# x loaded in two pieces by blocks, its first statistics taken piece by piece, the count of small norms placed behind the narrow products, and one scaling of rows on GpSimd

## The chip, the cores and the metric

The kernel runs on one core of one Trainium2 chip. Its metric is the time of an execution on the device in microseconds (us). TensorE, VectorE, ScalarE and GpSimd are called PE, DVE, ACT and POOL in the profile; SP is the sync engine, which here only issues DMAs. PEld is the loading of weights on PE.

## What is computed

Four graph layers on x (3327 nodes, 64 features) and a sparse adjacency matrix, each followed by x = layernorm(x + layer(x)). Only the start and layer 1 bear on this change. Cut to that:

```
def _L0_gnn_ref(t, x, A):
    outer = R_CONST * jnp.sum(x * (A @ x), axis=1, keepdims=True)
    return F_CONST - B_CONST * x - outer          # + x, then a layernorm
def _L1_gnn_ref(x, adj, att_W, att_b):
    x_tan = _logmap0(x, C)
    left  = x_tan @ att_W[:D] + att_b
    right = x_tan @ att_W[D:]
    adj_att = jax.nn.sigmoid(left + right.T) * adj
    x_local = _logmap(x[:, None, :], x[None, :, :], C)
    support_t = jnp.einsum('ij,ijd->id', adj_att, x_local)
    return _proj(_expmap(x, support_t, C), C)
```

The terms of layer 0 that are the same for all features of a node vanish in its layernorm, so layer 0 costs only the centring and the variance of x, and no pass over the adjacency matrix. Layer 1 needs a logarithm and a sigmoid for every pair of nodes.

## The kernel before, in words

**Tiles.** The nodes are padded to 3328 = 26 blocks of 128. A block lies on the 128 partitions; `x0`, `xc` (x less its mean) and `lj` hold 26 slots of 64 features each, 1664 numbers per partition. Slot 2c holds block c and slot 2c+1 block c+13, so that a pair of slots can be transposed as one 128x128 square. So "the even slots" are the first 13 blocks and "the odd slots" the last 13.

**The start (L105 to L214, and L1202 to L1287).** Two DMAs bring x, the first 13 blocks on SP's queue and the last 13 on ACT's (L106). SP then issues short columns (`attw_dg`, `attb_sb`), two rows of blocks of the adjacency matrix (`keep`, L144) and weights. POOL and DVE build constants. PE fills the time with matmuls into `idle` whose result nobody reads (L1206, three of them, two instructions each since the type is float32). When x is there, each engine follows the order in which the code is written (`manual_schedule`):

- DVE: row sums of the even slots and of the odd (L1212), then `xc` of the even and of the odd (L1214), later the row sums of the squares (L1243), then the small statistics `vq`, `low`, `lows`, `root`, `t`, `r2`, `lf`, `rb`, `gas` on 128x26 numbers (L1244 to L1286).
- POOL: `lj`, each feature less the last one, from `x0` for the even slots and from `xc` for the odd ones (L1220).
- PE: 13 transposes of x in four groups of 4, 4, 4 and 1 (L1231); in the second group also `pw` (L1236), the centred attention weights. Then 13 products `pr` of a transposed block with the 4 columns of weights (L1258, two instructions each), with a matmul into `idle` after the first and the last group (L1264).
- ACT: copies of the transposes out of PSUM to `xT` (L1240); in the second group first a copy of `pw` and the two squares of `xc` (L1239).

**The count.** `lows` counts, per partition, the nodes whose variance is under a bound; a matmul with ones (L1256, `n_low`) adds them over partitions, DVE turns the sum into an integer `flag` (L1272), and every engine reads that into a register and branches on it (L2097, L2098): layer 1 is `near_sphere` where no node is below, and a general path otherwise. `n_low` stands in PE's order before the last group of `pr`, and `flag` in DVE's before `t`, `r2`, `lf`, `rb` and `gas`.

**Layer 1's start (L1520 to L1600).** On DVE `scaled` (L1540) multiplies `lj` by `gas`, slots 18 to 25, then 10 to 17, then 0 to 9, with `rows_of_i` (L1513) between. A copy of one number, `after` (L1554), makes POOL wait for the last of them. PE transposes `lf`, `lj` and `ri` (`left`, `right`, `turn`, `wrong`), and ACT and DVE copy these out (L1502) to `lb`, `ljT`, `riT`. Then a loop over 104 tiles (52 pairs): ACT takes a sigmoid of `lb` (L1360) and an arctangent of the products (L1396), POOL multiplies the sigmoid by the adjacency (L1365), DVE makes the weights `v` (L1407 to L1411), PE makes the products `pq` (L1387) and the sums `acc` (L1431). The first four pairs use adjacency blocks that are already in SBUF, the others are loaded by SP (`at`, L1334). The first pair's sigmoid and its multiplication are cut in two.

After the loop come the end of layer 1, and layers 2 and 3 (`layers`), bound by PE and by loads of the adjacency. The diff doesn't touch these.

Of the kernel before, what the change touches and what calls it, by code (L numbers as in the profile page):

```python
# [10 lines left out]
F32 = mybir.dt.float32  # L11
# [3 lines left out]
AF = mybir.ActivationFunctionType  # L15
ALU = mybir.AluOpType
AX = mybir.AxisListType
PSUM = bass.MemoryType.PSUM

P = 128  # L20
# [3 lines left out]
D = 64  # L24
CW = 416
HALF = NP // 2
NBH = NB // 2
# [55 lines left out]
def kernel(  # L83
# [11 lines left out]
    nc = tc.nc  # L95
# [6 lines left out]


    x0 = xpool.tile([P, NB, D], F32, tag="x", name="x0")
    for h, queue in enumerate((nc.sync, nc.scalar)):  # L105
        queue.dma_start(  # L106
            x0[:, h::2, :], x_in[h * HALF : (h + 1) * HALF].rearrange("(c p) d -> p c d", p=P)
        )

    ident = const.tile([P, P], F32, name="ident")  # L110
    make_identity(nc, ident)
    lj = const.tile([P, NB, D], F32, name="lj")
# [9 lines left out]
    ones = const.tile([P, 1], F32, name="ones")  # L122
# [19 lines left out]
    def keep(blocks):  # L142
        for jb in blocks:
            nc.sync.dma_start(kept[jb], adjT[jb * P : (jb + 1) * P, :])  # L144
# [53 lines left out]
    center_4 = center.unsqueeze(1).to_broadcast([P, 4, P])  # L198
# [30 lines left out]
    def stat(tag):  # L229
        return small.tile([P, NB], F32, tag=tag, name=tag)  # L230
# [43 lines left out]
    def by_half(v):  # L274

        return v.rearrange("p (n h) d -> p n h d", h=2)
# [900 lines left out]
    with tc.tile_pool(name="l1", bufs=1) as l1:  # L1177

        def l1_stat(name):
            return l1.tile([P, NB], F32, name=name)  # L1180
# [5 lines left out]
        s, inv_s, gas, lf, rb = (l1_stat(name) for name in ("s", "inv_s", "gas", "lf", "rb"))  # L1186
# [6 lines left out]
        xc = xpool.tile([P, NB, D], F32, tag="x", name="xc")  # L1193
        vec, sca = nc.vector.tensor_tensor, nc.vector.tensor_scalar
        stt = nc.vector.scalar_tensor_tensor
        with tc.tile_pool(name="l1a", bufs=1) as l1a, tc.tile_pool(
            name="l1ap", bufs=1, space=PSUM
        ) as l1ap:
            v = l1a.tile([P, NB], F32, name="v")
            sums = l1a.tile([P, NB], F32, name="sums")  # L1200
            sq = l1a.tile([P, NB, D], F32, name="sq_c")
            xT = l1a.tile([P, HALF], F32, name="xT_0")  # L1202

            idle = l1ap.tile([P, 4 * P], F32, name="idle")
            for _ in range(3):
                nc.tensor.matmul(idle, ident, center_4, start=True, stop=True)  # L1206

            pw = l1ap.tile([P, 4], F32, name="pw")
            attw_c = l1a.tile([P, 4], F32, name="attw_c")
            halves = (slice(0, None, 2), slice(1, None, 2))  # L1210
            for h in halves:
                nc.vector.tensor_reduce(sums[:, h], x0[:, h, :], axis=AX.X, op=ALU.add)  # L1212
            for h in halves:
                stt(  # L1214
                    xc[:, h, :], sums[:, h].unsqueeze(2).to_broadcast([P, NBH, D]), -1.0 / D,
                    x0[:, h, :], op0=ALU.mult, op1=ALU.add,
                )
            for h, c in zip(halves, (x0, xc)):

                nc.gpsimd.tensor_tensor(  # L1220
                    lj[:, h, : D - 1], c[:, h, : D - 1],
                    c[:, h, D - 1 : D].to_broadcast([P, NBH, D - 1]), ALU.subtract,
                )

            pr = l1ap.tile([P, NBH, 2, 2], F32, name="pr")
            turned = []
            for i, g in enumerate(range(0, NBH, 4)):
                n = min(4, NBH - g)
                pt = l1ap.tile([P, 4 * P], F32, tag="pt", bufs=4, name=f"pt_x_{g}")
                for k in range(n):  # L1230
                    nc.tensor.transpose(  # L1231
                        pt[:, k * P : (k + 1) * P],
                        by_half(x0)[:, g + k].rearrange("p h d -> p (h d)"), ident,
                    )
                if i == 1:
                    nc.tensor.matmul(pw, center, attw_dg, start=True, stop=True)  # L1236
                    nc.scalar.copy(attw_c, pw)
                    for h in halves:
                        nc.scalar.activation(sq[:, h, :], xc[:, h, :], AF.Square)  # L1239
                nc.scalar.copy(xT[:, g * P : (g + n) * P], pt[:, : n * P])  # L1240
                turned.append((g, n))
            for h in halves:
                nc.vector.tensor_reduce(v[:, h], sq[:, h, :], axis=AX.X, op=ALU.add)  # L1243
            sca(vq[:, 1], v, 0.81 / D, LN_EPS, ALU.mult, ALU.add)  # L1244
            sca(vq[:, 0], v, MIN_VAR, None, ALU.max)
            sca(vq[:, 2], v, 0.81 / D - 0.81, LN_EPS, ALU.mult, ALU.add)

            low = stat("low")
            stt(low, v, NEAR_VAR, real, op0=ALU.is_lt, op1=ALU.mult)
            lows = small.tile([P, 1], F32, tag="lows", name="lows")  # L1250
            nc.vector.tensor_reduce(lows, low, axis=AX.X, op=ALU.add)
            root = l1a.tile([P, 2, NB], F32, name="root")
            n_low = l1ap.tile([1, 1], F32, name="n_low")
            for i, (g, n) in enumerate(turned):
                if i == 3:
                    nc.tensor.matmul(n_low, lows, ones, start=True, stop=True)  # L1256
                for k in range(g, g + n):
                    nc.tensor.matmul(  # L1258
                        pr[:, k].rearrange("p h t -> p (h t)"), xT[:, k * P : (k + 1) * P],
                        attw_c, start=True, stop=True,  # L1260
                    )
                if i in (0, 3):
                    w = 2 if i else 4
                    nc.tensor.matmul(  # L1264
                        idle[:, : w * P], ident, center_4[:, :w], start=True, stop=True
                    )
            nc.scalar.activation(root, vq[:, :2], AF.Sqrt)
            nc.scalar.activation(warm, ones, AF.Sigmoid)
            nc.vector.reciprocal(root, root)
            t = l1a.tile([P, 2, NB], F32, name="t")  # L1270
            vec(t, vq[:, :2], root, ALU.mult)
            nc.vector.tensor_copy(flag, n_low)  # L1272
            vec(t, t, root, ALU.mult)
            stt(r2, t, -3.0, root, op0=ALU.add, op1=ALU.mult)
            prs = pr.rearrange("p n h t -> p (n h) t")
            stt(lf, prs[:, :, 0], -0.5 * LOG_NORM, r2[:, 0], op0=ALU.mult, op1=ALU.mult)
            stt(rb, prs[:, :, 1], -0.5 * LOG_NORM, r2[:, 0], op0=ALU.mult, op1=ALU.mult)

            nc.vector.reciprocal(rq, vq[:, 1:])
            sca(rb, rb, attb_sb, None, ALU.add)  # L1280
            sca(s, r2[:, 1], -0.45, None, ALU.mult)
            vec(g1, vq[:, 2], rq[:, 0], ALU.mult)
            vec(ga, vq[:, 1], rq[:, 1], ALU.mult)
            vec(gas, ga, s, ALU.mult)
            sca(lj[:, :, D - 1], ga, 2.0, -1.0, ALU.mult, ALU.add)
            sca(aa, g1, -1.0, 1.0, ALU.mult, ALU.add)  # L1286
        in_order.close()  # L1287

        def near_sphere(mT, ljT_0, xm, sq_e, t_e):
# [3 lines left out]
            with tc.tile_pool(name="n1", bufs=1, reuse_waits="tile") as n1, tc.tile_pool(  # L1293
                name="n1w", bufs=2, reuse_waits="tile"
            ) as n1w, tc.tile_pool(
                name="n1c", bufs=1, space=PSUM, reuse_waits="tile"
# [43 lines left out]
                pqs, accs, changes, sums = {}, {}, [], []  # L1340
# [170 lines left out]
                def rows_of_i(first, last):  # L1511
                    sl = slice(2 * first, 2 * last)
                    stt(  # L1513
                        ri[:, sl, : D - 1], xc[:, sl, : D - 1], -2.0,
                        gas[:, sl].unsqueeze(2).to_broadcast([P, sl.stop - sl.start, D - 1]),
                        op0=ALU.mult, op1=ALU.mult,
                    )
# [11 lines left out]
                with tc.manual_schedule(  # L1529
# [4 lines left out]
                ):  # L1534
                    copy = nc.vector.tensor_copy
                    keep((NB - 3, NB - 4))
                    def scaled(b, n):

                        sl = slice(2 * b, 2 * (b + n))
                        vec(  # L1540
                            lj[:, sl, : D - 1], lj[:, sl, : D - 1],
                            gas[:, sl].unsqueeze(2).to_broadcast([P, 2 * n, D - 1]), ALU.mult,
                        )
# [4 lines left out]
                    rows_of_i(4, 8)  # L1548
                    scaled(5, 4)
                    rows_of_i(8, NBH)  # L1550
                    scaled(0, 5)

                    after = n1.tile([P, 1], F32, name="after")
                    nc.gpsimd.tensor_copy(after, lj[:, 0, :1])  # L1554
                    spread_a, spread_b = bank(0, left, 0, 4), bank(1, left, 13, 4)
                    spread_a()
                    spread_b()
# [2 lines left out]
                    start = attention(0)  # L1560
# [38 lines left out]
                    for t in range(len(tiles)):  # L1599
# [23 lines left out]
                        if t == len(tiles) - 3:  # L1623
                            pq = n1q.tile([P, 2, 512], F32, tag="pq", name="pq_early")
                            pm = pq[:, :, : 3 * (P + 2)].rearrange("p a (k w) -> p a k w", k=3)
                            for b in range(6):
                                nc.tensor.matmul(
                                    pm[:, b // 3, b % 3], mT[:, b * P : (b + 1) * P], all_m,
                                    start=True, stop=True,
# [524 lines left out]
```

## Time and profile before

| | us |
|---|---|
| three runs: median (lowest to highest) | 500.58 (498.72 to 500.65) |
| the profiled execution | 499.99 |
| its span | 498.2 |
| x asked for, first used by DVE, both halves used by PE | 0.81, 6.25, 7.14 |
| `n_low` on PE, `flag` on DVE | 14.53, 14.76 |
| PE's first instruction of layer 1, ACT's first, first arctangent | 16.37, 17.59, 24.52 |
| first loads of layer 2's stream, after the pair loop | 192.13 |

Times within an execution count from the span's start. A busy share of a stage says little by itself: what is read is which wait ended last ahead of an instruction. In a row of the timeline the columns are the start, the time to the end of the last of the instructions that are merged in the row, the engine, the line, what it writes and reads, and in brackets how long the engine had been idle and what ended that. Matmuls overlap, so the distance of two starts, not a duration, tells their pace.

### The profile page before, as it was taken

The numbers are of one execution on the slowest core, as the hardware profiler recorded it, in microseconds if no ns is written. First come the engines' busy times: TensorE is split into PE (matmuls) and PEld (weight loads), VectorE is DVE, ScalarE is ACT, GpSimd is POOL, SyncE is SP. The second block draws the span as 40 slices with busy tenths as digits, with TensorE's granted clock in tenths as the row PEclk, the third lists the DMA queues.
The fourth block names the chain that finished last, engine by engine and source line by source line (L and its number), as shares of the span: only waits on it lengthen the run. The fifth ranks groups of instructions, "written<-read, shape, count | busy, mean of one in ns | idle before, by whom it ended". The sixth has DMA issues, their size and how long they took to land. (4 is left out here: it accounts for less than half of the span.)

```text
span 498.2 us, 7727 instructions
## 1 busy us (share of the span) xinstructions
PE 480.3 (96%) x2865; PEld 220.4 (44%) x2865; DVE 349.5 (70%) x602; ACT 266.1 (53%) x377; POOL 192.1 (39%) x171
## 2 busy tenths in 40 slices
PE   7999999999999999999999999999999999999992
PEld 4733333333333338643333353333345554455551
DVE  6788888878888887995363322656239998788744
ACT  4799999999999985300000000000016885657541
POOL 4299999989999991000000000000242154000000
PEclk9799999999999998999999999999999999999996
DMA  9888988887888278899999019998987699949001
GB/s 278 340 284 285 328 265 274 273 272 259 283 274 277 72 285 312 365 402 428 424 425 379 0 22 393 430 362 325 414 337 236 224 331 364 392 162 357 3 1 43
DMA packets 34202, 139.20 MB, mean 279 GB/s; under 512 B 11263, under 2 KB 13041, under 8 KB 29035
## 3 DMA queue, kind: packets, MB, share of 16 engines
q1 hardware_dynamic: 30603, 137.41, 73.8%
q0 software_dynamic: 1216, 0.63, 0.6%
q10 hardware_dynamic: 2336, 0.58, 0.6%
q8 instruction: 24, 0.39, 0.3%
q14 instruction: 23, 0.19, 0.1%
HBM read 136.93 MB, written 1.04 MB: 277 GB/s over the span
## 5 line engine op out<-in xcount | busy, mean ns | idle before, releaser
L1365 POOL TENSOR_TENSOR sg<-sg,at 128x832 f32<-128x832 f32 x88 | 131.4, 1517 | 7.7 <-ACT sg L1360 3.7
L517 PE MATMUL cnt<-at_l,lj 128*64 128x416 f32 x496 | 90.8, 515 | 0.8 <-DMA at_l<-in_adjT 0.8
L1360 ACT ACTIVATE sg<-lb,rb 128x1664 f32<-128x1664 f32 (+1 forms) x53 | 88.1, 1664 | 0.0
L1387 PE MATMUL pq<-riT,ljT 64*128 64x416 f32 x416 | 87.4, 536 | 0.2
L1431 PE MATMUL acc<-v,lj 128*64 128x416 f32 x416 | 85.2, 525 | 0.0
L1396 ACT ACTIVATE pq<-pq 128x832 f32<-128x832 f32 x104 | 83.8, 851 | 1.8 <-issue 1.6
L630 ACT ACTIVATE x<-cnt 128x416 f32<-128x416 f32 x8 | 4.1, 517 | 144.7 <-PE cnt L517 144.7
L669 ACT ACTIVATE w<-cnt 128x416 int16<-128x416 f32 x136 | 63.9, 522 | 25.3 <-PE cnt L651 23.8
L1411 DVE SCALAR_TENSOR_TENSOR v<-pq,sg 128x832 f32<-128x832 f32 x52 | 53.3, 1025 | 19.0 <-ACT pq L1396 18.6
L464 POOL DMA_DIRECT2D t_rows<-tb x4 | 2.7, 720 | 151.0 <-DVE tb L462 151.0
L1387 PEld LDWEIGHTS pq<-riT,ljT 64*128 64x128 f32 x416 | 35.5, 186 | 49.8 <-ACT pq L1396 30.6
L517 PEld LDWEIGHTS cnt<-at_l,lj 128*64 128x64 f32 x496 | 34.3, 137 | 51.0 <-issue 48.4
L882 PE MATMUL acc<-w,s 128*128 128x416 bf16 x208 | 53.1, 339 | 0.0
L1431 PEld LDWEIGHTS acc<-v,lj 128*64 128x64 f32 x416 | 26.1, 136 | 52.3 <-issue 48.2
L667 DVE TENSOR_SCALAR w<-cnt 128x416 int16<-128x416 f32 x72 | 41.6, 587 | 10.0 <-PE cnt L651 7.8
L517 PE MATMUL cnt<-kept,lj 128*64 128x416 f32 x224 | 41.6, 514 | 0.0
L651 PE MATMUL cnt<-mask,tri 128*128 128x416 bf16 x136 | 35.5, 339 | 1.8 <-ACT w L669 0.9
L368 DVE TENSOR_SCALAR mask<-ah 128x1664 bf16<-128x1664 f32 x34 | 35.5, 1060 | 2.3 <-DMA ah<-in_adjT 2.3
L1408 DVE SCALAR_TENSOR_TENSOR pq<-pq,sg 128x416 f32<-128x416 f32 x52 | 31.2, 600 | 1.8
L445 DVE TENSOR_SCALAR tm<-at_l 128x1664 bf16<-128x1664 f32 x16 | 15.7, 1023 | 22.9 <-PE t L452 20.9
L1407 DVE SCALAR_TENSOR_TENSOR v<-pq,sg 128x416 f32<-128x416 f32 x52 | 30.2, 581 | 0.0
L1035 POOL DMA_DIRECT2D out<-hid x1 | 0.5, 502 | 74.5 <-DVE hid L1040 74.5
(320 smaller groups left out, 523.5 us busy)
## 6 DMA issues: line engine op xcount, KB each, us to landing
at_l<-in_adjT SPq DMA_DIRECT2D x27, 1664.0 KB
at<-in_adjT SPq DMA_DIRECT2D x44, 832.0 KB
ah<-in_adjT SPq DMA_DIRECT2D x34, 832.0 KB
kept<-in_adjT SPq DMA_DIRECT2D x7, 1664.0 KB
bt_l<-in_adjT SPq DMA_DIRECT2D x6, 1664.0 KB
lb<-lf_rows SPq DMA_DIRECT2D x2, 384.0 KB
mask<-t_rows SPq DMA_DIRECT2D x34, 3.2 KB
ljT<-ljT SPq DMA_DIRECT2D x4, 128.0 KB
```

Of the source, the lines that this page charges most:

```text
L368: nc.vector.tensor_scalar(mask[q], ahead.pop(q), 0.0, None, ALU.not_equal)
L517: nc.tensor.matmul(acc[c][h * D : (h + 1) * D, :], hw[:, slot(jb), :], blocks[jb][:, o : o + CW], start=c not in begun, stop=last, skip_gr ...
L651: nc.tensor.matmul(cnt[c][e], tri, mask[q][:, of], start=True, stop=True, skip_group_check=True,)
L667: nc.vector.tensor_scalar(to, of, 0.0, None, ALU.max)
L669: nc.scalar.activation(to, of, AF.Relu)
L882: nc.tensor.matmul(acc[h, c][:, e, :], s12[:, slot(jb)].rearrange("p t d -> p (t d)"), ws[q, c, e], start=first, stop=last,)
L1360: nc.scalar.activation(sg[:, :, of], lbs[:, :, of], AF.Sigmoid, bias=rb[:, sl : sl + 1])
L1365: nc.gpsimd.tensor_tensor(sg[:, h, of], sg[:, h, of], at[:, h, of], ALU.mult)
L1387: nc.tensor.matmul(pq[:, h, :], ljT[h != jb // NBH][rows, of], riT[rows, ch * CW : (ch + 1) * CW], start=True, stop=True,)
L1396: nc.scalar.activation(pqs[t], pqs[t], AF.Arctan, bias=ANGLE_FIRST, scale=ANGLE_STEP)
L1411: stt(w, pq, ANGLE_REST, sg, op0=ALU.add, op1=ALU.mult)
L1431: nc.tensor.matmul(accs[cp, ci][h * D : (h + 1) * D, :], lj[:, slot(jb), :], w[:, h, :], start=(jb == orders[cp][0]), stop=(jb == orders[c ...
```

## The change

x comes in two pieces by blocks: blocks 0 to 6 and 13 to 19 (slots 0 to 13), then blocks 7 to 12 and 20 to 25 (slots 14 to 25), each piece as one DMA on SP and one on ACT. Sums, `xc`, `lj`, the squares and their sums go by these pieces instead of by even and odd slots, with the sum and `xc` of the first piece ahead of the second's, and the second square behind the second copy to `xT`. Two of three `idle` matmuls ahead of x are dropped. `n_low` stands behind the last group of `pr`. `scaled(0, 5)` goes to POOL, and `after` is dropped.

```diff
-    for h, queue in enumerate((nc.sync, nc.scalar)):
-        queue.dma_start(
-            x0[:, h::2, :], x_in[h * HALF : (h + 1) * HALF].rearrange("(c p) d -> p c d", p=P)
-        )
+    x_parts = (slice(0, 7), slice(7, NBH))
+    for s in x_parts:
+        for h, queue in enumerate((nc.sync, nc.scalar)):
+            o = h * HALF
+            queue.dma_start(
+                x0[:, 2 * s.start + h : 2 * s.stop : 2, :],
+                x_in[o + s.start * P : o + s.stop * P].rearrange("(c p) d -> p c d", p=P),
+            )
...
-            for _ in range(3):
-                nc.tensor.matmul(idle, ident, center_4, start=True, stop=True)
+            nc.tensor.matmul(idle, ident, center_4, start=True, stop=True)
...
-            halves = (slice(0, None, 2), slice(1, None, 2))
-            for h in halves:
-                nc.vector.tensor_reduce(sums[:, h], x0[:, h, :], axis=AX.X, op=ALU.add)
-            for h in halves:
+            pieces = [slice(2 * p.start, 2 * p.stop) for p in x_parts]
+            for sl in pieces:
+                nc.vector.tensor_reduce(sums[:, sl], x0[:, sl, :], axis=AX.X, op=ALU.add)
                 stt(
-                    xc[:, h, :], sums[:, h].unsqueeze(2).to_broadcast([P, NBH, D]), -1.0 / D,
-                    x0[:, h, :], op0=ALU.mult, op1=ALU.add,
+                    xc[:, sl, :],
+                    sums[:, sl].unsqueeze(2).to_broadcast([P, sl.stop - sl.start, D]), -1.0 / D,
+                    x0[:, sl, :], op0=ALU.mult, op1=ALU.add,
                 )
-            for h, c in zip(halves, (x0, xc)):
+            for sl, c in zip(pieces, (x0, xc)):
...
-                    for h in halves:
-                        nc.scalar.activation(sq[:, h, :], xc[:, h, :], AF.Square)
+                if i in (1, 2):
+                    sl = pieces[i - 1]
+                    nc.scalar.activation(sq[:, sl, :], xc[:, sl, :], AF.Square)
                 nc.scalar.copy(xT[:, g * P : (g + n) * P], pt[:, : n * P])
...
-            for h in halves:
-                nc.vector.tensor_reduce(v[:, h], sq[:, h, :], axis=AX.X, op=ALU.add)
+            for sl in pieces:
+                nc.vector.tensor_reduce(v[:, sl], sq[:, sl, :], axis=AX.X, op=ALU.add)
...
-                if i == 3:
-                    nc.tensor.matmul(n_low, lows, ones, start=True, stop=True)
                 for k in range(g, g + n):
                     nc.tensor.matmul(
                         pr[:, k].rearrange("p h t -> p (h t)"), xT[:, k * P : (k + 1) * P],
                         attw_c, start=True, stop=True,
                     )
+                if i == 3:
+                    nc.tensor.matmul(n_low, lows, ones, start=True, stop=True)
...
-                    def scaled(b, n):
+                    def scaled(b, n, engine=nc.vector):
...
-                        vec(
+                        engine.tensor_tensor(
...
-                    scaled(0, 5)
-
-                    after = n1.tile([P, 1], F32, name="after")
-                    nc.gpsimd.tensor_copy(after, lj[:, 0, :1])
+                    scaled(0, 5, nc.gpsimd)
```

More of the change, by code (lines that the diff above doesn't have):

```diff
@@ L1204 @@
             idle = l1ap.tile([P, 4 * P], F32, name="idle")
-            for _ in range(3):
-                nc.tensor.matmul(idle, ident, center_4, start=True, stop=True)
+            nc.tensor.matmul(idle, ident, center_4, start=True, stop=True)
             pw = l1ap.tile([P, 4], F32, name="pw")
             attw_c = l1a.tile([P, 4], F32, name="attw_c")
-            halves = (slice(0, None, 2), slice(1, None, 2))
-            for h in halves:
-                nc.vector.tensor_reduce(sums[:, h], x0[:, h, :], axis=AX.X, op=ALU.add)
-            for h in halves:
-                stt(
-                    xc[:, h, :], sums[:, h].unsqueeze(2).to_broadcast([P, NBH, D]), -1.0 / D,
-                    x0[:, h, :], op0=ALU.mult, op1=ALU.add,
+            pieces = [slice(2 * p.start, 2 * p.stop) for p in x_parts]
+            for sl in pieces:
+                nc.vector.tensor_reduce(sums[:, sl], x0[:, sl, :], axis=AX.X, op=ALU.add)
+                stt(
+                    xc[:, sl, :],
+                    sums[:, sl].unsqueeze(2).to_broadcast([P, sl.stop - sl.start, D]), -1.0 / D,
+                    x0[:, sl, :], op0=ALU.mult, op1=ALU.add,
                 )
-            for h, c in zip(halves, (x0, xc)):
+            for sl, c in zip(pieces, (x0, xc)):
                 nc.gpsimd.tensor_tensor(
-                    lj[:, h, : D - 1], c[:, h, : D - 1],
-                    c[:, h, D - 1 : D].to_broadcast([P, NBH, D - 1]), ALU.subtract,
+                    lj[:, sl, : D - 1], c[:, sl, : D - 1],
+                    c[:, sl, D - 1 : D].to_broadcast([P, sl.stop - sl.start, D - 1]),
+                    ALU.subtract,
                 )
```

## The prediction

> **What bounds the kernel now.** I read the page first. PE is busy 480.3 of 498.2 us, and its first slice of 12.5 us is the emptiest but the last. All edits lie in the first 22 us, so I read the timeline from 0 to 28 us, then the stretches of 1 us for PE's clock, the waits, and last the pair loop, to see whether a gain at the start reaches the end.
>
> The timeline of the start:
>
> ```profile
> 6.25 1.95 DVE L1212 TENSOR_REDUCE sums<-x 128x13 f32<-128x832 f32 x2 [3.20 <-DMA x<-in_x]
> ...
> 7.14 1.09 PE L1231 MATMUL pt_x<-ident,x 128*128 128x128 f32 x8 [0.60 <-DMA x<-in_x]
> ...
> 8.11 1.95 DVE L1214 SCALAR_TENSOR_TENSOR xc<-sums,x 128x832 f32<-128x832 f32 x2
> ...
> 10.09 1.96 DVE L1243 TENSOR_REDUCE v<-sq_c 128x13 f32<-128x832 f32 x2
> ...
> 10.89 1.22 ACT L1240 COPY xT<-pt_x 128x512 f32<-128x512 f32 x3
> 11.52 3.08 PE L1258 MATMUL pr<-attw_c,xT 128*128 128x4 f32 x16 [0.81 <-ACT xT L1240]
> ...
> 14.53 0.19 PE L1256 MATMUL n_low<-ones,lows 128*1 128x1 f32 x2
> ...
> 14.76 0.15 DVE L1272 CAST flag<-n_low 1x1 int32<-1x1 f32 x1 [1.38 <-PE n_low L1256]
> ...
> 16.40 1.94 PE L1446 MATMUL prep_left<-ident,lf 128*128 128x128 f32 x8
> ```
>
> DVE works without a hole from 6.25 to 12.05. `lows` is done at 12.73 (the row at 12.55 takes 0.18), but `n_low` runs at 14.53: PE was still in the narrow products, which began when ACT, held by both squares, copied `xT` at 10.89. So the wait that ends last ahead of the branch is PE's queue, not the statistics. Behind `flag`, DVE still has `t`, `r2`, `lf`. PE's work for layer 1 begins at 16.40, ACT's at 17.59, and from 18.38 ACT has no hole up to the loop.
>
> The stretches of 1 us (columns: sum of the stretch, PE, PEld, DVE, ACT, POOL, granted clock, DMA share, GB/s):
>
> ```profile
> 8.00:9.00 1.00, 1.00 (x13) 1.00 (x10) 1.00 (x2) 0.55 (x2) 0.00 (x0) 1.00 0.99 399
> ...
> 13.00:14.00 1.00, 1.00 (x6) 1.00 (x7) 0.34 (x2) 0.99 (x2) 0.00 (x0) 0.50 1.00 426
> ...
> 17.00:18.00 1.00, 1.00 (x7) 0.96 (x6) 0.76 (x3) 0.41 (x1) 0.00 (x0) 0.50 0.63 186
> ...
> 20.00:21.00 1.00, 1.00 (x18) 0.85 (x16) 1.00 (x2) 1.00 (x3) 0.00 (x0) 1.00 1.03 439
> ```
>
> PE runs at half clock from 12.08 to 18.92 (from the shares in 12:13 and 18:19, both 0.54). So 16 product instructions take 3.08 us (0.19 each), against 8 in 0.95 (0.12) at full clock.
>
> The loop, at its only hitch on POOL (timelines of POOL, DVE and ACT):
>
> ```profile
> 51.02 17.75 POOL L1365 TENSOR_TENSOR sg<-sg,at 128x832 f32<-128x832 f32 x12 [1.13 <-DMA at<-in_adjT]
> ...
> 54.02 1.02 DVE L1411 SCALAR_TENSOR_TENSOR v<-pq,sg 128x832 f32<-128x832 f32 x1 [0.39 <-POOL sg L1365]
> ...
> 51.41 1.68 ACT L1360 ACTIVATE sg<-lb,rb 128x1664 f32<-128x1664 f32 x1
> ```
>
> ACT has no hole here and repeats every 3.14 us (48.28, 51.41, 54.58): it sets the pace, POOL with 2.99 is just under it. 52 pairs give 163 us; whatever moves the first arctangent (24.52) moves the loop's end.
>
> **x in two pieces.** x is 852 KB. The stretches from 1 to 6 us moved 5, 200, 241, 255 and 263 KB, so all of it has moved by about 5.6, and the first piece (7/13, 459 KB) by about 4.05. DVE saw SP's half at 6.25, 0.6 behind its bytes; PE saw ACT's half at 7.14, 1.5 behind, since SP's adjacency loads had begun to share. First piece: 4.65 by the one, 5.55 by the other; I take 4.9, nearer to the undisturbed. The second piece stays at 7.1 to 7.2. Two more issues cost about 0.5 us each on ACT and SP; ACT's pushes the table load at 1.35, covered by ACT's 4.98 us of idling; SP's pushes `attw_dg` (wanted by `pw` at 8.07, asked for at 1.32) and the adjacency rows (wanted at 21.57). Without cover each would cost its 0.5.
>
> DVE's four passes of x take 0.975 us per 832 elements: 1.05 for 896, 0.90 for 768. From 4.9, piece one is centred at 7.0. Piece two then begins at its landing, 7.2, and is centred at 9.0 instead of 10.06. A first piece later than 5.1 would begin to cost, a sooner one brings nothing.
>
> But PE's second group of transposes holds block 7, of the second piece, and `pw` stands behind it. So PE waits to 7.2, `pw` is done at about 7.7, and ACT's order then is: `attw_c` 7.8, square one 8.0 to 8.95 (0.915 x 896/832), `xT` 8.95 to 9.5, square two 9.5 to 10.35, `xT` to 10.9 and 11.2. DVE's second sum of squares ends at 11.3 instead of 12.05, so `lows` at about 11.95: 0.75 sooner. `xT` of the second group comes at 9.5 instead of 11.4. POOL's `lj` (1.55 each) lies beside all this and has 9.7 us to spare.
>
> **Two idle matmuls fewer.** Nobody reads `idle`; what they change is PE's clock. The trace: their weights load at 3.21, 4.06, 4.91 and 5.52, so 0.85 apart and then 0.61; at 0.43 for full clock, the step falls at 5.28. The drop at 12.08 and the rise at 18.92 are 6.80 and 13.64 later, two and four times 3.41. The Trainium skill, "TensorE: Matmul & The Clock Gate", Part 1, says that half clock is the default, that a busy window of 3.4 us releases it and an idle one takes it back, and that windows run free of the kernel's start. The trace agrees with the step, but differs in what is busy: from 12.08 to 15.5 PE is recorded busy all through with narrow products, and the clock stays at 0.50. By the rule alone, one matmul of 1.7 us (2.19 to 3.9) fills no window and the clock stays low to about 12: dropping them costs. By the rows, the transposes may raise it: at half clock they take 0.225 each (8 of `left` in 1.94 us, first to last start 1.57), 13 of them nearly 3 us in the window 5.28 to 8.69, and a window of transposes and `idle` (15.5 to 18.92) did raise it. So two cases:
>
> - *Full clock from 8.7.* Transposes end at 8.5, `pr` of group one 8.7 to 9.6, `idle` to 10.5, then groups two, three, four by 0.12 each: 11.4, 12.4, 12.6 with part of it at half clock. `n_low` at about 12.7 instead of 14.53: 1.8 sooner.
> - *Half clock to 12.1 or longer.* `pr` one 8.9 to 10.4 (8 x 0.19), `idle` 1.7 to 12.1, groups two and three 3.1 to 15.2, group four 0.4, `n_low` at about 15.6: 1.1 later.
>
> **The count behind the products.** It puts two product instructions, 0.25 to 0.4 us, ahead of `n_low`; already in both sums. Queued behind `flag` on DVE: `t`, `r2`, `lf`, `rb`, `gas`; behind the branch: all engines. The products themselves are needed by `lf` anyway, so they lose nothing.
>
> **From there to the loop.** In the first case `lf` comes 1.8 sooner (13.8) and PE begins at 14.4, but PE is at half clock: its 8 + 4 + 6 + 4 + 16 preparations, of which before the last 22 ran at full clock behind 18.92, now mostly run slow. Right and left (18 x 0.225) end at 18.5 instead of 19.8, turn and wrong, partly slow, at about 20.2 instead of 21.23. ACT's copy of `wrong` moves from 21.58 to about 20.4: 1.2 us are left of 1.8. In the second case `left` begins at about 16.9 instead of 16.4; everything is 0.5 to 1.1 later, I take 0.7.
>
> **A scaling on POOL.** The trace has no such product on POOL with a broadcast factor in layer 1's start; the near rows are `lj` on POOL with a broadcast operand (1551 ns for 819, so 1.19 us for 630) and 1945 ns for 832 (1.47). I take 1.2, beside 0.81 on DVE. It starts as soon as `gas` and the branch are there (16.6 before), ends by about 18, and its readers (`right` of blocks 0 to 4 on PE) come at 21.77: 3 us of cover; without it, up to 0.7. DVE's gain of 0.81 at 20.43 goes into a wait, since its next work waits for PE's `first_turn` (0.63). Without `after`, POOL can start its first pair at 20.0, when the sigmoid is there, instead of 21.57; but the first `v` at 25.51 waited for ACT, not POOL. A gain is excluded by that, a loss through DVE and POOL reading SBUF together by the loop, where DVE's row of 832 takes 1.025 beside POOL and 1.018 at 8.11: 0 for both.
>
> **The sum.** The likeliest is the first case: 1.2 us off the profiled 499.99 (span 498.2, and 1.8 around it) gives 498.8. That execution is 0.6 below the median of 500.58; against the median it is 499.4.
>
> **The rivals.**
>
> 1. *PE stays at half clock* (place: `n_low` in PE's queue; price: 0.7 us; it decides when transposes do not count as enough work in the window in which they fall, so when the clock at 9 us is 0.50). For it: the rule, and the free windows. Against: 15.5 to 18.92. Time 501.3, slower than before. If the half clock lasts one window longer, to 22.3, turn, wrong and the rest cost another 1.5 or so: 502.8. Chance 0.27 together.
> 2. *The gain is swallowed at 51 us.* POOL waits there 1.13 us for a load behind which SP had stood. SP's loads follow DVE's copies (27.20), so they should move along; if DMA, at a share of 1.03 from 46 to 54, does not, POOL waits 1.2 longer and ACT's pace breaks. Time 500.6. Chance 0.13.
> 3. *More than I took.* If the window from 12.1 to 15.5, which then holds `idle` and half of `left`, raises the clock at 15.5, the preparations run at full clock: 2.5 us, 498.0. Chance 0.13.
> 4. *Nothing comes of it*: the first piece lands no sooner than 6, since both queues' rows are moved mixed. Then DVE has two pieces in a row as before, and only the earlier `xT` remains: 0.3 or so, 500.3. Chance 0.10.
>
> The forecast has 0.37.
>
> **How the numbers follow.** All cases lie between 498.0 and 502.8; runs of the kernel before differ by 1.9 us. Half a per cent (2.5 us, 498.1 and 503.1) is about what a measurement of this kernel can tell from no change. Faster by more: rival 3, most of it, and a share of the forecast with a low median, 0.14. Slower by more: the long half clock, 0.08. Within: 0.78. Range 497.6 to 502.0.
>
> **What would show it.** First `sums` at about 4.9 and `xc` of piece two done by 9.0; granted clock at 9 us; `n_low` at 12.7 (15.6 in rival 1); ACT's copy of `wrong` at 20.4; the first arctangent at about 23.3; POOL's scaling with about 1.2 us, done ahead of 18; POOL's wait near 50 still about 1.1; layer 2's first loads at about 190.9. I am wrong if the branch stops depending on `n_low`, if the loop has another pace than 3.14, or if the difference arises behind 200 us, where nothing was changed.

## The result, and the profile after

The changed kernel takes 503.39 us (median of 6, 502.53 to 503.85) against 499.37 us of the kernel before, run beside it. The ratio is 1.0081, with a 95% interval of 1.0064 to 1.0097: about 4.0 us slower. That is outside the range given (497.6 to 502.0) and on the other side. The profiled execution took 503.29 us, with a span of 501.6. The ratios here and below leave out executions more than 1.5% above the fastest of their kernel; there are two, both in the last experiment.

The timeline of the start, in the changed kernel:

```profile
5.22 1.08 DVE L1215 TENSOR_REDUCE sums<-x 128x14 f32<-128x896 f32 x1 [2.17 <-DMA x<-in_x]
5.25 2.23 PE L1235 MATMUL pt_x<-ident,x 128*128 128x128 f32 x8 [0.98 <-DMA x<-in_x]
5.28 1.66 POOL L1223 TENSOR_TENSOR lj<-x 128x882 f32<-128x882 f32 x1 [1.81 <-DMA x<-in_x]
...
6.34 1.54 DVE L1216 SCALAR_TENSOR_TENSOR xc<-sums,x 128x896 f32<-128x896 f32 x1
...
8.78 0.96 DVE L1216 SCALAR_TENSOR_TENSOR xc<-sums,x 128x768 f32<-128x768 f32 x1
...
12.35 3.84 PE L1261 MATMUL pr<-attw_c,xT 128*128 128x4 f32 x18
...
16.12 0.19 PE L1266 MATMUL n_low<-ones,lows 128*1 128x1 f32 x2
...
16.35 0.15 DVE L1277 CAST flag<-n_low 1x1 int32<-1x1 f32 x1 [3.41 <-PE n_low L1266]
...
17.57 1.94 PE L1451 MATMUL prep_left<-ident,lf 128*128 128x128 f32 x8
...
18.27 1.24 POOL L1545 TENSOR_TENSOR lj<-lj,gas 128x630 f32<-128x630 f32 x1 [7.01 <-DVE aa L1291]
18.74 1.31 DVE L1545 TENSOR_TENSOR lj<-lj,gas 128x504 f32<-128x504 f32 x1 [0.47 <-DVE aa L1291]
...
20.11 1.12 PE L1473 MATMUL first_right<-ident,lj 128*128 128x128 f32 x4 [0.60 <-DVE lj L1545]
...
21.23 2.50 POOL L1370 TENSOR_TENSOR sg<-sg,kept 128x832 f32<-128x832 f32 x1 [1.71 <-ACT sg L1365]
...
21.84 2.56 DVE L1518 SCALAR_TENSOR_TENSOR mT<-xc,gas 128x630 f32<-128x630 f32 x1
...
23.29 1.98 PE L1483 MATMUL first_wrong<-ident,lj 128*64 128x128 f32 x16
```

Three rows of the kernel before, for comparison:

```profile
17.24 0.68 DVE L1540 TENSOR_TENSOR lj<-lj,gas 128x504 f32<-128x504 f32 x1 [0.49 <-DVE aa L1286]
...
19.70 0.81 DVE L1513 SCALAR_TENSOR_TENSOR mT<-xc,gas 128x630 f32<-128x630 f32 x1
...
20.14 1.09 PE L1478 MATMUL first_wrong<-ident,lj 128*64 128x128 f32 x16
```

x does come a microsecond sooner (5.22 instead of 6.25), and `lows` is there at 12.28 instead of 12.73. But `n_low` stands at 16.12 instead of 14.53. All 18 narrow product instructions since 12.35 go at 0.21 us each, and `first_wrong` takes 1.98 us for the same 16 instructions that took 1.09. PE is at half clock until 25.33 us. Twice in layer 1's start a DVE instruction beside a POOL one lasts far longer than its twin: `lj` 1.31 instead of 0.68, and the row product 2.56 instead of 0.81.

How the delay grows: `flag` is 1.59 us later, PE's first `prep_left` 1.17 (in both kernels it stands behind the last idle matmul and not behind `lf`; the other 0.42 of `n_low` and `flag` is their new place, behind two products), `first_right` 1.97, the end of `first_wrong` 4.04 (25.27 against 21.23), the first arctangent 3.73 (28.25 against 24.52), layer 2's first loads 3.7 (195.8 against 192.13). So all of it is there by the first arctangent, at 28 us, and the pair loop and the layers behind it pass it on nearly whole: the two profiled executions differ by 3.30 us.

The granted clock in stretches of 1 us can't be read here. In the changed kernel it says:

```profile
14.00:15.00 1.00, 1.00 (x7) 1.00 (x6) 0.00 (x0) 0.00 (x0) 0.00 (x0) 1.00 0.83 193
...
17.00:18.00 1.00, 0.90 (x4) 0.47 (x3) 0.96 (x8) 0.00 (x0) 0.00 (x0) 1.00 0.00 0
18.00:19.00 1.00, 1.00 (x7) 1.00 (x6) 0.53 (x4) 0.25 (x1) 0.73 (x1) 1.00 1.15 200
```

It shows 1.00 where 8 transposes take 1.94 us, exactly what they took in the kernel before at a granted 0.50. The column shows 1.00 until a first change is recorded. The changes themselves lie in the trace with their times: the first is the rise to full clock, at 25.33 us in the changed kernel and at 5.26 in the kernel before. The pace of like instructions agrees with these times, not with the column, so the sign that the prediction named for 9 us could not be read there. Where a time of a rise is given below, it is from these records.

### The profile page after: what moved, and what is told of

Same layout as the page of the kernel before. It is cut to its first block, busy times and chain, and to the rows that moved or that the text cites. A ratio compares the mean times of both kernels' runs of the same rounds, so it can differ in the third digit from the quotient of the medians.

```text
span 501.6 us, 7725 instructions
## 1 busy us (share of the span) xinstructions
PE 483.8 (96%) x2861; PEld 223.9 (45%) x2861; DVE 352.1 (70%) x601; ACT 266.7 (53%) x377; POOL 193.4 (39%) x171
## 4 chain that ended last, share of the span: by engine, by line
PE 82%; DVE 6%; DMA 5%; ACT 1%; issue 1%; SPq 0%; DVEq 0%; ACTq 0%
PE cnt L521 26%; PE pq L1392 16%; PE acc L1436 16%; PE cnt L655 6%; PE acc L886 6%; PE acc L903 3%; DMA at_l<-in_adjT 3%; PE t L456 2%; DMA mask<-t_rows 2%; PE both L756 1%; PE cnt L512 1%; DVE mask L372 1%; PE pn_l L407 1%; PE pr_o L946 1%; PE pe L1724 1%
## 5 line engine op out<-in xcount | busy, mean ns | idle before, releaser
L468 POOL DMA_DIRECT2D t_rows<-tb x4 | 4.1, 1058 | 150.9 <-DVE tb L466 150.9
```

## The experiments

Theories, stated before the runs. *Clock*: the two dropped `idle` matmuls leave PE at half clock, and most of the loss comes from that. *Port*: DVE is held up by POOL since the scaling moved. *Pieces*: the cut of x itself tears holes in PE's work. *Order*: `n_low` behind the products delays the branch. In each group of runs the kernel before ran on the same chip, with medians of 499.95, 499.89 and 500.37; its executions spread from 497.75 to 502.11. So ratios are compared. One per cent is 5.0 us. The ratios stand here as they are on record; the quotient of the two medians differs from them by up to 0.2% (one idle matmul: medians 2.6 us apart, ratio 1.0073 or 3.6 us), so no size below is known better than to about 1 us.

### Undoing parts of the change, and single parts of it

**The change with three idle matmuls again.**

```diff
-            nc.tensor.matmul(idle, ident, center_4, start=True, stop=True)
+            for _ in range(3):
+                nc.tensor.matmul(idle, ident, center_4, start=True, stop=True)
```

> The changed kernel with all three idle matmuls ahead of x again, all else as changed. Clock theory (the two idle matmuls that were dropped kept PE at half clock from the start to about 25.5 us, and most of the 4.0 us lost come from that): full clock from some point near 5 to 9 us, n_low at about 13 instead of 16.1, the time 500.5 or less, so 2.5 to 4 us under the changed kernel. Port theory (most of the loss is DVE held up by POOL): less than 1 us comes back, 502.5 or more. Pieces theory (cutting x leaves holes in PE's work and the clock is lost whatever comes first): half clock again from about 9 us to 25 us, 502.5 or more.

Measured: 501.12 us, ratio 1.0034 (1.0018 to 1.0049). Of 0.81% more than half, 0.47% or 2.3 us, is gone (the two intervals leave 0.24 to 0.70%). The rise comes at 5.64, and `n_low` runs at 12.63 instead of 16.12:

```profile
6.57 1.04 PE L1236 MATMUL pt_x<-ident,x 128*128 128x128 f32 x8
...
12.63 0.19 PE L1267 MATMUL n_low<-ones,lows 128*1 128x1 f32 x2
```

The bound of 500.5 was missed by 0.6, so by the medians the two dropped matmuls are the larger part, not the whole. In this kernel a second half-clock stretch came later, from 12.46 to 22.70 (its stretches 12:13 and 22:23 show 0.73 and 0.65), and the preparations fell into it.

**The change with the last scaling on DVE again.**

```diff
-                    scaled(0, 5, nc.gpsimd)
+                    scaled(0, 5)
+
+                    after = n1.tile([P, 1], F32, name="after")
+                    nc.gpsimd.tensor_copy(after, lj[:, 0, :1])
```

> The changed kernel with the last scaling of rows on DVE again and POOL waiting for it (the copy called after), one idle matmul, all else as changed. Clock theory: at most 0.9 us comes back (first_right waited 0.6 us for DVE, whose first scaling took 1.31 beside POOL instead of 0.68), 502.5 to 503.4. Port theory: 2 us or more come back, 501.4 or less.

Measured: 502.88 us, ratio 1.0068 (1.0044 to 1.0092). By the ratios about 0.65 us comes back, inside what the clock theory allowed, but the intervals overlap: it is not told from nothing. Port as the main cause (501.4 or less) falls. In the profiled execution DVE's first scaling takes 0.68 again, `first_right` hardly waits (0.2 us), and the rise comes at 21.66 instead of 25.33.

**The kernel before with one idle matmul.** The first diff the other way round, applied to the kernel before.

> The kernel before with one idle matmul ahead of x instead of three, and nothing else changed. Clock theory: half clock to about 22 to 25 us, narrow products slow from the first one, n_low about 1 us later than 14.5, the time 501.5 to 503, so 2 to 3.5 us slower than before. Pieces theory: the unbroken transposes from 7.1 us on keep or bring the clock, within 0.7 us of before.

Measured: 502.52 us, ratio 1.0073 (1.0049 to 1.0098): 3.6 us by the ratio, 2.6 by the medians, for two matmuls whose result nobody reads. Its timeline:

```profile
7.13 1.97 PE L1230 MATMUL pt_x<-ident,x 128*128 128x128 f32 x8 [2.87 <-DMA x<-in_x]
...
13.70 3.41 PE L1257 MATMUL pr<-attw_c,xT 128*128 128x4 f32 x16
...
17.04 0.19 PE L1255 MATMUL n_low<-ones,lows 128*1 128x1 f32 x2
...
17.27 0.15 DVE L1271 CAST flag<-n_low 1x1 int32<-1x1 f32 x1 [3.63 <-PE n_low L1255]
```

The first 8 transposes take 1.97 us instead of 1.09, with x in unbroken halves, and `n_low` is 2.5 us later. The rise comes at 21.73. The unbroken transposes did not raise the clock: the pieces theory falls for this part, and so does my forecast's step.

**The kernel before with only the scaling moved to POOL**, `after` dropped.

> The kernel before with only the last scaling of rows moved to POOL and without the copy called after. Port theory in its weak form, as part of the whole: DVE's first scaling takes 1.3 instead of 0.68 and one of the row products waits for POOL's multiplication, 0.5 to 0.9 us slower than before, 500.0 to 500.3. Port theory as the main cause: 2 us or more slower. The prediction's own step: no difference, since its readers come 3 us later.

Measured: 500.59 us, ratio 1.0018 (1.0003 to 1.0033): 0.9 us slower by the ratio (0.15 to 1.65), 0.6 by the medians. The weak form of the port theory holds; "no difference" falls, by a little. Its timeline shows the price at once:

```profile
15.53 1.24 POOL L1540 TENSOR_TENSOR lj<-lj,gas 128x630 f32<-128x630 f32 x1 [3.93 <-DVE aa L1286]
16.01 1.30 DVE L1540 TENSOR_TENSOR lj<-lj,gas 128x504 f32<-128x504 f32 x1 [0.48 <-DVE aa L1286]
...
17.37 1.12 PE L1468 MATMUL first_right<-ident,lj 128*128 128x128 f32 x4 [1.39 <-DVE lj L1540]
```

POOL is done at 16.77, and 0.54 us later, at 17.31, DVE: that fits a DVE that moved data only as POOL let go. PE waited 1.39 us for it. With DVE's scaling at 0.68, the same wait was 0.60 (only the count moved) and 0.81 (two idle matmuls) in profiles in which `prep_left` was done as early, so some 0.6 to 0.8 of the 1.39 is the port.

**Only the pieces**: as the change, but with three idle matmuls, the scaling on DVE and the count in its old place.

```diff
+                if i == 3:
+                    nc.tensor.matmul(n_low, lows, ones, start=True, stop=True)
                 for k in range(g, g + n):
...
-                if i == 3:
-                    nc.tensor.matmul(n_low, lows, ones, start=True, stop=True)
```

(From the changed kernel; the other two parts are undone as in the first two diffs of this section.)

> Of the change only the two pieces of x and the statistics by pieces: three idle matmuls ahead of x, the last scaling on DVE with POOL waiting, the count ahead of the last products. Clock and port theories together: the pieces cost nothing, flag up to 1.5 us sooner where PE has full clock until then, but PE's preparations then fall more into the half clock; 0 to 1 us faster than before (498.9 to 499.9). Pieces theory: slower than before by 0.5 us or more, since holes between the pieces cost PE its clock.

Measured: 500.47 us, ratio 1.0009 (0.9995 to 1.0022): not told from no change. No gain, and no 0.5 us of loss that could be shown. The trace shows why: `n_low` runs at 12.43, where it came at 13.30 and 13.45 in two profiles with x in halves and full clock up to it. Then the clock is at half from 13.82 to 20.64, under PE's preparations (`prep_left` 1.94), and the first arctangent comes at 24.08, 0.44 us sooner than in the kernel before.

**Only the count moved**, in the kernel before: the diff above the other way round.

> The kernel before with only the count moved behind the last narrow products. The prediction's step: n_low 0.25 to 0.4 us later, and as PE's next work waits for an idle matmul that stands behind both, at most 0.3 us slower, not told from no change. A theory that the order matters as such (every engine waits for the branch): 0.5 us or more slower.

Measured: 499.99 us, ratio 1.0008 (0.9993 to 1.0022): not told from no change. The order theory falls as a cause of its own. In the changed kernel the order costs `n_low` the two product instructions now ahead of it, at half clock 0.42 us.

### The port by itself

**The scaling on POOL, but kept from DVE's first scaling**: POOL begins when DVE's second row product is written, and its first multiplication waits for the last row product.

```diff
...
-                    scaled(0, 5)
+                    gate = n1.tile([P, 1], F32, name="gate")
+                    nc.gpsimd.tensor_copy(gate, ri[:, 15, :1])
+                    scaled(0, 5, nc.gpsimd)
...
-                    nc.gpsimd.tensor_copy(after, lj[:, 0, :1])
+                    nc.gpsimd.tensor_copy(after, ri[:, 25, :1])
```

> The kernel before with the last scaling on POOL, but held back by a POOL copy that reads what DVE's second row product wrote, and POOL's first multiplication held back until DVE's last row product is written. Port theory (an instruction of DVE with two inputs in SBUF waits for the whole of a POOL instruction): the collision is moved from DVE's first scaling to its second, whose reader is late; first_right waits no more, and the time is that of before, within 0.3 us. If POOL is too slow or too late for its readers, slower by 0.5 us or more as with the scaling moved freely.

Measured: 499.78 us, ratio 1.0001 (0.9990 to 1.0012). With the collision moved, the same scaling on the same engine costs nothing that could be told:

```profile
18.76 0.68 DVE L1540 TENSOR_TENSOR lj<-lj,gas 128x504 f32<-128x504 f32 x1
...
19.35 0.81 DVE L1513 SCALAR_TENSOR_TENSOR mT<-xc,gas 128x630 f32<-128x630 f32 x1
19.45 1.81 POOL L1540 TENSOR_TENSOR lj<-lj,gas 128x630 f32<-128x630 f32 x1
```

This time DVE began first and kept its 0.81; POOL, 0.10 behind, took 1.81 instead of 1.24. I had expected DVE's second scaling to be hit; it had just ended. Whoever begins second waits for the other's end.

### The clock by itself, and a version that gains

**The kernel before with two idle matmuls.** `range(2)` in place of `range(3)`.

> The kernel before with two idle matmuls ahead of x instead of three. Clock theory: a matter of whether a whole window of 3.4 us is filled: two matmuls of 1.7 us at half clock fill one only in some executions, so times fall into two groups, near 499.9 and near 502.5, or lie between; the median between 500.2 and 502.5. If the time depended on the amount of idle work smoothly: 501.2 with no wider spread.

Measured: 501.23 us, ratio 1.0032 (1.0015 to 1.0049). The 22 executions fall into two groups with nothing between 501.54 and 502.90: 13 from 499.91 to 501.54, and 9 from 502.90 to 504.17. The five executions with one idle matmul, 502.35 to 503.52, lie near the second group. That two matmuls suffice in some executions and not in others, as windows that run free of the kernel would have it, fits this better than "half the price for half the work"; but the only profile is of the first group (500.36, rise at 5.07), so the clock of the second was not seen.

**The pieces with more idle work**: to the pieces alone, 256 columns behind the second group of products, and 512 in place of 256 behind the last.

```diff
-                if i in (0, 3):
-                    w = 2 if i else 4
+                if i in (0, 1, 3):
+                    w = (4, 2, 0, 4)[i]
```

> The pieces alone (as in the kernel with only the pieces), with more work for nobody to keep PE's clock: an idle matmul of 256 columns also behind the second group of narrow products, and 512 columns instead of 256 behind the last. Clock theory: fewer microseconds at half clock between 12 and 22 us, ACT's copy of the wrong squares under 21 us, 0.5 to 2 us faster than before (498 to 499.4). If the added work delays the count more than the clock gives back: within 0.5 us of the pieces alone, or slower.

Measured: 498.63 us, ratio 0.9972 (0.9962 to 0.9981), the one version shown to be faster than the kernel before, by 1.4 us, with 22 executions from 496.61 to 499.69. In the profiled one PE has full clock from 5.71 on, through all the preparations:

```profile
11.57 0.95 PE L1264 MATMUL pr<-attw_c,xT 128*128 128x4 f32 x8
...
12.63 0.19 PE L1262 MATMUL n_low<-ones,lows 128*1 128x1 f32 x2
...
14.20 1.06 PE L1452 MATMUL prep_left<-ident,lf 128*128 128x128 f32 x8
...
16.42 0.66 PE L1474 MATMUL first_right<-ident,lj 128*128 128x128 f32 x4 [1.16 <-DVE lj L1546]
...
18.10 1.09 PE L1484 MATMUL first_wrong<-ident,lj 128*64 128x128 f32 x16
```

`prep_left` takes 1.06 us instead of 1.94, and `first_wrong` ends at 19.19, 2.0 us ahead of the kernel before. PE now waits for DVE (1.16). The first arctangent comes at 22.18, 2.34 us sooner. But part of that is lost near 50 us, where POOL waits again:

```profile
50.65 19.65 POOL L1371 TENSOR_TENSOR sg<-sg,at 128x832 f32<-128x832 f32 x13 [3.12 <-DVE pq L1414]
```

The wait there was 1.13 us in the kernel before and is 3.12 now. POOL's multiplication waits there on several conditions; its row names DVE, in the kernel before it named the load. The last arctangents start at 183.78, only 1.86 us ahead of 185.64: 0.5 of 2.34 us is swallowed at this place.

**The kernel before with the same added idle work**, x in halves.

> The kernel before, x in halves, with the added idle matmuls (256 columns behind the second group of narrow products, 512 instead of 256 behind the last). If the clock alone makes the gain of the pieces with more idle: 498.6, a ratio near 0.997. If the earlier statistics of the pieces are needed for it: 499.3 to 499.9, a ratio of 0.999 or more, since DVE's statistics end 0.3 to 0.7 us later than with pieces.

Measured: 500.61 us, ratio 1.0016 (1.0002 to 1.0030): 0.8 us slower by the ratio, 0.2 by the medians. That the clock alone makes the gain falls; the time lies above the second expectation's 499.9 too, though inside its "ratio of 0.999 or more". In its profiled execution (501.48, one of the longer) PE stood idle for 0.76 us ahead of the second group, waiting for `xT` behind both squares, and the clock fell to half at about 14.08. Then the longer idle matmul ran at half clock itself, 2.06 us, and `prep_left` came at 16.77. Idle work that doesn't hold the clock is paid twice: the same 512 columns took 1.10 at 9.87. With this idle work added, pieces and halves are 0.44% apart (0.9972 and 1.0016, each against the kernel before on its own chip), where without it pieces were not told from no change. So with it the pieces pay; whether by their earlier statistics or because the clock stays up was not separated.

**The whole change with three idle matmuls and the added idle work.**

> The whole change (pieces, count behind the products, scaling on POOL) with three idle matmuls ahead of x and the added ones. Clock and port theories: the pieces with more idle (498.6) and the price of the scaling on POOL (0.7 to 1.4, as DVE is now what PE waits for), 499.3 to 500.0. If the scaling on POOL is worth something once the clock is kept: 498.6 or less.

Measured: 499.42 us, ratio 0.9986 (0.9968 to 1.0004), inside the first expectation, but told neither from the kernel before nor from the pieces with more idle work (0.9972, 0.9962 to 0.9981). That the scaling on POOL still takes away from the gain is the likely reading, not shown: in the profiled execution the clock was at half from 13.62 to 17.04.

**The pieces with one idle matmul ahead of x and one in the hole** between the first and the second group of transposes, and the added ones.

```diff
+                if i == 0:
+                    nc.tensor.matmul(idle, ident, center_4, start=True, stop=True)
                 if i == 1:
```

> The pieces alone with the added idle matmuls, but with one idle matmul ahead of x as in the change and one behind the first group of transposes, in the hole in which PE waits for the second piece. Clock theory: 1.7 us at the start fill no window, but the transposes, the idle matmul and the first products fill one or the next, so full clock from about 9 to 12 us; 499 to 501. If work ahead of x is what counts and nothing later raises the clock before the preparations: half clock to 22 us, 502 or more.

Measured: 499.63 us, ratio 0.9991 (0.9976 to 1.0006), in the range expected. In the profiled execution the rise comes at 8.36:

```profile
6.29 1.91 PE L1240 MATMUL idle<-both_m,ident 128*128 128x512 f32 x2
...
7.99 0.78 PE L1235 MATMUL pt_x<-ident,x 128*128 128x128 f32 x4
...
9.33 0.95 PE L1265 MATMUL pr<-attw_c,xT 128*128 128x4 f32 x8
```

Up to there PE's work differs from that of the changed kernel by the matmul in the hole alone. But 3 of the 22 executions took 503.98 to 506.3, and the ratio is without two of them. Perhaps the clock did not come up in those; no profile shows it.

## Why the prediction was wrong, point by point

**The step that failed first: "a window of transposes and `idle` (15.5 to 18.92) did raise it".** I took from that row the case that the 13 transposes bring full clock from 8.7, with `n_low` at 12.7. They did not, neither in pieces (the changed kernel: half clock to 25.33, `n_low` at 16.12) nor in halves (one idle matmul in the kernel before: 8 of them took 1.97, half clock to 21.73). What raised the clock in the kernel before at 5.26 was a window nearly full of 512-column matmuls, which began at 2.19.

Transposes as such can raise it. In the changed kernel the rise at 25.33 stands behind 3.41 us in which PE ran nothing but transposes, without a gap of more than 0.2; so it does with the scaling on DVE again (21.66). What the row did not show is that 13 transposes, about 3 us of them, fill a window where they fall. Counted back from the rises in steps of 3.41, an estimate from one execution each, they did not. In the changed kernel that window is 4.85 to 8.26: x comes at 5.24, and the weight loads stand still for 0.40 us ahead of block 7 and 0.21 ahead of `pw`. In halves it is 8.08 to 11.49, and its last 1.2 us are narrow products. My row, 15.5 to 18.92, held 0.8 us of idle matmul at its start and a gap of 0.1. I had worked out the wait for block 7 and not carried it over into the clock; with an idle matmul in that place the clock came up at 8.36.

The Trainium skill's rule that I had weighed ("TensorE: Matmul & The Clock Gate", Part 1: half clock is the default, a busy window of 3.4 us releases it) stood against the change, and for the start it was right: one matmul, recorded from 2.19 to 4.27, fills no window. The two groups of times with two idle matmuls fit it. But recorded busy is not what counts. In the changed kernel PE is recorded busy without a gap from 8.0 to 17.4, mostly with narrow products; by the rule alone the clock would have come up by 14.8 (two windows of 3.41, an estimate), and it did not until 25.33.

**Rival 1 was what happened, in its long form, and bigger.** It had `n_low` at 15.6; it came at 16.12. It had 502.8 for a half clock to 22.3; it lasted to 25.33. I had given both forms together 0.27 and then drawn the range's end at 502.0, short of a case I had worked out.

**That the loop excludes a loss through DVE and POOL reading SBUF together was false.** The loop's DVE row that ran at 1.025 beside POOL reads one operand from PSUM (`pq`), the other from SBUF. At the start both operands are in SBUF, and 0.68 became 1.31, 0.81 became 2.56. The Trainium skill says just this ("SBUF — State Buffer", Who interferes with whom): a DVE instruction with two inputs in SBUF contends with a POOL instruction that reads SBUF, and the one that issues second is blocked for the other's whole length. Both directions are measured here (1.31 and 2.56 on DVE, 1.81 on POOL). The step "0 for both" should have read 0.6 for the first scaling, as PE's `right` waits for it. Measured are 0.9 us alone (0.15 to 1.65) and, not told from nothing, 0.65 within the change. It would also explain `after`, which I had read as a mere order; that was not tried. That the wait of 0.60 at 19.5 to 20.1 also kept a window of transposes from filling, so that the rise came at 25.33 and not near 21.9, is likely from the profile without that wait (21.66), one execution each.

**The pieces.** First sums were forecast at 4.9 and came at 5.22; the first piece was centred at 7.88, not 7.0. Of that 0.9, 0.3 is the landing; 0.5 is the same blocking, since `xc` of the first piece (1.54) now meets POOL's `lj` from `x0`, which in the kernel before ended at 7.85, ahead of it. So piece two was centred at 9.74 instead of 9.0, and `lows` came 0.45 us sooner instead of 0.75. The whole is worth nothing that could be told (ratio 1.0009), as half clock under the preparations took back what `n_low` gained.

**The count behind the products**: right in size by the trace (0.25 to 0.4 forecast, 0.42 at half clock) and in cause; in the time it is not told from nothing.

**The scaling's duration on POOL**: 1.2 forecast, 1.24 measured. That its readers come late was right too; what I did not price was what it does to DVE beside it.

**Rival 2** (the gain swallowed near 50 us) could not show in a slower kernel: the wait there was 0.98. It did show where a gain existed: 0.5 us of 2.34.

**The parts against the whole.** By the ratios the parts alone cost 3.6 us (idle), 0.9 (scaling), and 0.4 each that can't be told from nothing (pieces, count): 5.3 in all against 4.0 measured. By the medians it is 2.6, 0.6, 0.6 and 0.1, or 3.9. Within the change, the idle matmuls are worth 2.3. So neither that the parts overlap nor that they just add up is shown. What is left with the idle matmuls back (1.7) is the sum of the other three within their intervals.

What stays open is how much work a window must hold. With two idle matmuls, the window ahead of the rise at 5.07 was empty for its first 0.53 us; with only the count moved, the rise came at 8.40, and the window before the last, empty for its first 0.61, had not sufficed. That puts the bound between about 82 and 85% of a window, for matmuls of 512 columns, an estimate from two executions. Open too is why the added idle work held the clock with pieces and not with halves in the profiled executions; the hole of 0.76 us is a likely reason, only argued.

## What to carry to other kernels

Work that nobody reads can be what holds PE's clock: before taking it out, find the clock's steps in the pace of like instructions, and ask which window keeps it up afterwards. Before moving an elementwise instruction to POOL, look at what DVE does beside it then: with both operands in SBUF one of the two waits for the other's end, and a row from a place with an operand in PSUM proves nothing. And where a worked-out rival lies outside the range, either its chance or the range is wrong.

## What the runs showed of the hardware that was not expected

- The granted-clock column shows 1.00 until the first change is recorded: 8 transposes took 1.94 us at a shown 1.00 and at a shown 0.50. Here that first change was the rise to full clock.
- Narrow products (4 columns) do not raise the clock though PE is recorded busy all the time: at 0.50 from 12.08 to 15.5 in the kernel before, and from 12.35 to 16.12 in the changed one. Transposes raise it where they fill 3.41 us (21.9 to 25.33 in the changed kernel); 13 of them, about 3 us, did not.
- The clock changes at steps of 3.41 us whose place differs between executions of nearly the same kernel. With three idle matmuls the rise came at 5.26 to 8.40. In eight of nine such profiles the fall came 6.83 us after it, at 12.1 to 15.2, and only the pieces with more idle work had none. The stretches of half clock behind a fall lasted 3.41 (two profiles), 6.83 (six, one of them with two idle matmuls) or 10.24 us (one).
- The kernel before spread from 497.75 to 502.11 us over 67 executions. That these steps are the cause is likely from the two groups of times, but was not shown for it by itself.
